# A four-layer graph network on one core: VectorE, GpSimd and SyncE in the order of the program, and one PSUM bank for each stage

## The chip, the core and the metric

The kernel runs on one core of one Trainium2 chip. The metric is the device time of one execution in microseconds, the median of several. The core has a matrix engine (TensorE, PE in the profile, with its weight loads PEld), a vector engine (VectorE, DVE), a scalar engine for activation functions (ScalarE, ACT), GpSimd (POOL), and SyncE (SP), which issues the DMAs. Each engine takes its own queue of instructions in order; semaphores tie them together. Matmuls write to PSUM, which has eight banks of 128 x 512 float32.

## The reference

The input is 64 graphs of 256 nodes with 128 features, `x` (64, 256, 128), and a 0/1 adjacency `adj` (64, 256, 256). Four layers follow each other, each with a residual and a layer norm:

```python
# layer 0: the maximum over the neighbours j of relu(p[i] + q[j] + b)
pre = p[:, :, None, :] + q[:, None, :, :] + b
h = jax.nn.relu(pre) * adj[..., None]
x = _layernorm(x + jnp.max(h, axis=2))
# layer 1: three elu branches, two products with adj, tanh
x = _layernorm(x + jnp.tanh(jnp.einsum('bnk,ok->bno', upd, W_upd) + b_upd))
# layer 2: two graph convolutions with D^-1/2 (adj + I) D^-1/2, elu between
x = _layernorm(x + out)
# layer 3: the sum over the neighbours j of gelu(layernorm(m_j[j] + m_i[i] + b1))
msg = jax.nn.gelu(_layernorm(pre, g1, be1), approximate=False)
agg = jnp.einsum('bijo,bij->bio', msg, adjacency)
x = _layernorm(x + _layernorm(jnp.concatenate([nodes, agg], -1) @ W2 + b2, g2, be2))
```

Layers 0 and 3 work on every edge. The kernel's sparse path handles them by sorting the nodes of a graph by degree and giving each node up to 40 slots for its neighbours.

## The kernel before, in words

**Four stages, pipelined over graphs.** All 64 graphs are unrolled. A graph goes through `first` (layer 0), `second` (layer 1), `third` (layer 2 and half of layer 3) and `last` (the rest of layer 3). In one round the kernel records `last` of graph g, `third` of g+1, `second` of g+2 and `first` of g+3 together. Each stage is a Python generator that stops at each `yield`; `together` always advances the stage that has done the smallest share of its steps, by the counts in `STAGES`. This gives the order in which instructions are recorded. A scheduler then reorders them for every engine, by its own estimate of when each could start, and puts in the waits.

**`first`** loads `xn` and `an`, makes `nz` and `diff` on DVE, transposes `nz` on PE into `aT` (copied by ACT), and counts neighbours (`pc`, `pd` in PSUM). From them come `kc`, `dg`, four Sign activations into `more` (L551), the place of each node (`place`, L556), and the permutation `perm` (L560, DVE). Matmuls with `perm` (L566) give `nzp`, then `rank` and `lack`, each a matmul and an ACT copy. `hot` (L629, DVE) is a 0/1 matrix of 4800 columns that says which node sits in which slot. The rows for the slots are gathered by three bf16 matmuls of `q3` with `hot` into a PSUM bank `bigp` (L665, L681 for the missing slots), and DVE folds the banks into `lanes` by the maximum (L492), ten banks for each half of the nodes. `permT` brings the maxima back (`m0`, L705 to L709), and a layer norm gives `x1`.

**`third` and `last`** gather in the same way for layer 3, in tiles of 1024 columns, ten for a graph. `sums_of` does one tile: gather on PE (L728), add the node's own term `dT` on DVE (L732, `pre`), square on ACT (L736), sum the squares over the features on PE (L743), copy them to `row` on ACT (L745), and write `row` to DRAM (`line`, L750). After two tiles, `vr` is read back with one variance for each edge (L762), brought to its inverse root, multiplied by `fu` (L769), written out (`scale_line`, L771), and later spread over all partitions by a DMA of 512 KB (`rs_s`, L828). `last` multiplies `pre` by `rs_s` (L839, DVE), applies Gelu (L841, ACT) and folds the sums (L492). The gather runs four tiles ahead of this (`AHEAD`), and `rs_s` two tiles ahead.

**Inverse roots** stand in five places: the variances `rs` of all layer norms, the degrees `dinv`, and `vr`. All call

```python
def inverse_root(t):
    nc.scalar.activation(t, t, AF.Sqrt)
    nc.vector.reciprocal(t, t)
```

ACT holds one table of functions at a time; where Sqrt, Exp and Gelu alternate, the built program has an ACT_TABLE_LOAD before the activation, shown under the line of the activation that follows.

**PSUM.** Four banks belong to the gathers (`bigp`, pool `ps_big`). The other four are one pool, `ps_mm`, under one name, `mm`, shared by all stages in turn.

Of the kernel before, what the change touches and what calls it, by code (L numbers as in the profile page):

```python
# [43 lines left out]
def kernel(  # L44
# [20 lines left out]
    half = consts.tile([P, N], F32, name="half")  # L65
    nc.vector.memset(half, 0.5)
# [4 lines left out]

    def inverse_root(t):

        nc.scalar.activation(t, t, AF.Sqrt)  # L74
        nc.vector.reciprocal(t, t)
# [81 lines left out]
    class Shared:  # L157


        def __init__(self, work, state, ps_mm):  # L160
            self.work, self.state, self.ps_mm = work, state, ps_mm

        def psum(self):
            return self.ps_mm.tile([P, 512], F32, name="mm")

        def layernorm(self, dst, src, g=None, be=None):

            st = self.work.tile([P, H, 6], F32, name="st", bufs=4)
            mv = self.work.tile([P, H, 2], F32, name="mv", bufs=4)
            for h in range(H):  # L170
                nc.vector.bn_stats(st[:, h], src[:, h])
                nc.vector.bn_aggr(mv[:, h], st[:, h])
            rs = self.work.tile([P, H], F32, name="rs", bufs=4)
            nc.vector.tensor_scalar(rs, mv[:, :, 1], EPS, None, ALU.add)
            yield
            inverse_root(rs)
            yield
            for h in range(H):
                if g is None:
                    nc.vector.tensor_scalar(  # L180
                        dst[:, h], src[:, h], mv[:, h, 0:1], rs[:, h:h + 1], ALU.subtract, ALU.mult
                    )
                else:
                    nc.vector.scalar_tensor_tensor(dst[:, h], src[:, h], mv[:, h, 0:1], g, ALU.subtract, ALU.mult)
                    nc.vector.scalar_tensor_tensor(dst[:, h], dst[:, h], rs[:, h:h + 1], be, ALU.mult, ALU.add)

        def elu(self, dst, t, twice=False):

            e = self.work.tile([P, 512], F32, name="elu_e")
# [6 lines left out]
            if twice:  # L196
                nc.vector.tensor_scalar(e, e, 1.0, None, ALU.min)
                nc.scalar.activation(e, e, AF.Exp, bias=minus1)
# [4 lines left out]
        def to_features(self, xn, name, bufs=None):  # L203

            pt = self.psum()
            for h in range(H):
                nc.tensor.transpose(pt[:, h * P:(h + 1) * P], xn[:, h], ident)
            t = self.state.tile([P, N], F32, name=name, **({"bufs": bufs} if bufs else {}))
            nc.scalar.copy(t, pt[:, :N])
            return t  # L210

# [3 lines left out]
        def layer_1(self, s, an, aT, x1):  # L215

            work, psum, elu = self.work, self.psum, self.elu
            xT = self.to_features(x1, "xT_1", 1)
# [6 lines left out]
            for h in range(H):  # L225
                nc.vector.tensor_add(io[:, h], pr[:, h * N:(h + 1) * N], b1_io)
            yield from elu(io, io)
# [5 lines left out]
            nc.vector.tensor_scalar(nd, pn[:, :N], b1_node, None, ALU.add)  # L233
            yield from elu(nd, nd)
# [16 lines left out]
            y = work.tile([P, H, P], F32, name="y", bufs=2)  # L251
            for h in range(H):
                nc.vector.tensor_add(y[:, h], pu[:, h * P:(h + 1) * P], b1_upd)
            nc.scalar.activation(y, y, AF.Tanh)
# [6 lines left out]
        def layer_2(self, s, aT, deg_of):  # L261
# [3 lines left out]
            deg = work.tile([P, H], F32, name="deg")  # L265
            deg_of(deg)
            nc.vector.tensor_scalar(deg, deg, 1.0, None, ALU.add)
            pos = work.tile([P, H], F32, name="pos")
            nc.vector.tensor_scalar(pos, deg, 0.0, None, ALU.is_gt)
            dinv = work.tile([P, H], F32, name="dinv")  # L270
            nc.vector.tensor_scalar(dinv, deg, 1e-30, None, ALU.max)
            inverse_root(dinv)
            yield
            nc.vector.tensor_mul(dinv, dinv, pos)
            for h in range(H):
                blk = aT[:, h, h * P:(h + 1) * P]
                nc.vector.tensor_add(blk, blk, ident)
            yield
            xT = self.to_features(x2, "xT_2", 1)
# [7 lines left out]
            for h in range(H):  # L287
                nc.vector.tensor_add(hs[:, h], ph[:, h * P:(h + 1) * P], b2[0])
            yield from elu(hs, hs, twice=True)
            yield  # L290
            for step in (1, 2):
                for h in range(H):
                    nc.vector.tensor_scalar(hs[:, h], hs[:, h], dinv[:, h:h + 1], None, ALU.mult)  # L293
# [17 lines left out]
                if step == 1:  # L311
                    yield from elu(hs, hs)
# [6 lines left out]
        def update(self, g, s, add_agg):  # L319
# [8 lines left out]
            y = self.work.tile([P, H, P], F32, name="y", bufs=2)  # L328
# [25 lines left out]
    def sparse(ctx):  # L354
        cs = ctx.enter_context(tc.tile_pool(name="cs", bufs=1))
        dram = ctx.enter_context(tc.tile_pool(name="dram", bufs=12, space=bass.MemoryType.DRAM))
        ps_mm = ctx.enter_context(tc.tile_pool(name="ps_mm", bufs=4, space=bass.MemoryType.PSUM))
# [32 lines left out]
        with tc.tile_pool(name="cs_prep", bufs=1) as pp:  # L390
# [21 lines left out]
            for t, slots in ((most, [w for s0, n, w in RECTS for _ in range(n)]), (least, SURE)):  # L412
# [7 lines left out]
                for hk in range(H):  # L420
                    pt = ps_mm.tile([P, 512], F32, name="mm")
# [7 lines left out]
            pt = ps_mm.tile([P, 512], F32, name="mm")  # L429
# [25 lines left out]
        sh = Shared(work, state, ps_mm)  # L455
        psum = sh.psum
# [37 lines left out]
        def split3(dst, src):  # L494

            r = work.tile([P, H, P], F32, name="rest")
            nc.scalar.copy(dst[:, 0], src)
# [3 lines left out]

        def first(g, s):

            xn = sh.node_tile("x0")
            nc.sync.dma_start(xn, x[ds(g, 1)].rearrange("b (h p) d -> p (b h) d", p=P))
            an = state.tile([P, H, N], F32, name="an")
            nc.sync.dma_start(an, adj[ds(g, 1)].rearrange("b (h p) j -> p (b h) j", p=P))
# [3 lines left out]
            nc.vector.scalar_tensor_tensor(diff, an, -1.0, an, ALU.add, ALU.mult)  # L511
            aT = state.tile([P, H, N], F32, name="aT", bufs=3)
            for hj in range(H):
                pt = psum()
                for hi in range(H):
                    nc.tensor.matmul(
                        pt[:, hi * P:(hi + 1) * P], nz[:, hi, hj * P:(hj + 1) * P], ident_b, start=True, stop=True
                    )
                nc.scalar.copy(aT[:, hj], pt[:, :N])
            nzT = as_bf16(aT)  # L520
            yield
            xT = sh.to_features(xn, "xT_0", 1)


            pd = psum()
            for h in range(H):
                cols = slice(h * N, (h + 1) * N)
                nc.tensor.matmul(pd[:, cols], many_b, nzT[:, h], start=True, stop=False)
                nc.tensor.matmul(pd[:, cols], ones_b[:1], down, start=False, stop=True)
# [9 lines left out]
            fl = work.tile([P, 1 + 2 * H * H], F32, name="fl")  # L539
            nc.scalar.activation(diff, diff, AF.Abs, accum_out=fl[:, 0:1])  # L540
            kc = work.tile([P, H, H], F32, name="kc")
            nc.vector.scalar_tensor_tensor(kc, pc, -1.0, down_c, ALU.mult, ALU.subtract)
            dg = state.tile([P, H], F32, name="dg", bufs=3)
            nc.vector.tensor_reduce(dg, pc, AX.X, ALU.add)
            s["dg"] = dg

            more = work.tile([P, H, H], F32, name="more")
            for h in range(H):
                for hi in range(H):
# [3 lines left out]
                    )  # L553
            yield
# [9 lines left out]
            for h in range(H):  # L564
                for hi in range(H):
# [3 lines left out]
                    )  # L569
            nzp = pair.tile([P, H, N], BF16, name="nzp")  # L570
            nc.scalar.copy(nzp, pz.rearrange("p (h n) -> p h n", h=H))
            permT = hold.tile([P, H, H, N], F32, name="permT")
            for h in range(H):
                pt = psum()
                for hk in range(H):
                    for hi in range(H):
                        nc.tensor.matmul(
                            pt[:, (hk * H + hi) * P:(hk * H + hi + 1) * P],
                            perm_b[:, h, hi, hk * P:(hk + 1) * P], ident_b, start=True, stop=True,
                        )  # L580
                nc.scalar.copy(permT[:, h].rearrange("p a n -> p (a n)"), pt)
# [3 lines left out]
            nc.tensor.matmul(pr, upto, nzp.rearrange("p h n -> p (h n)"), start=True, stop=True)  # L585
            rank = pair.tile([P, H, N], BF16, name="rank")
            nc.scalar.copy(rank, pr.rearrange("p (h n) -> p h n", h=H))
            pg = psum()
            nc.tensor.matmul(pg[:ROWS], ones_b[:, :ROWS], nzp.rearrange("p h n -> p (h n)"), start=True, stop=True)
            lack = hold.tile([ROWS, H, N], BF16, name="lack")  # L590
            nc.scalar.activation(
                lack, pg[:ROWS].rearrange("p (h n) -> p h n", h=H), AF.Relu, bias=part1[:ROWS], scale=-1.0
            )

            pf = psum()
            for h in range(H):
                for hk in range(H):
# [3 lines left out]
                    )  # L601
            yield
# [6 lines left out]
            lack_t = pair.tile([ROWS, H, g_n, g_w], BF16, name="lack_t")  # L609
            for h in range(H):  # L610
                nc.vector.tensor_mul(lack_t[:, h], tail, widen(lack[:, h, :g_w], g_n))
            s.update(an=an, aT=aT, perm=perm, permT=permT, lack=lack)

            full = pair.tile([ROWS, H, N], BF16, name="full")
            nc.vector.tensor_scalar(full, lack, 0.0, None, ALU.is_equal)
# [7 lines left out]
            yield  # L623

            hot = hold.tile([P, H, WIDTH], FP8, name="hot")
            for s0, n, w in RECTS[:-1]:
                for i in range(n):
# [4 lines left out]
                    if i % 4 == 3 or i == n - 1:  # L632
                        yield
# [9 lines left out]
            s["hot"] = hot  # L643

# [7 lines left out]
            q3 = work.tile([P, 3, H, P], BF16, name="q3")  # L652
            split3(q3, pq[:, :, 0])
            own = work.tile([P, H, P], F32, name="own")
            for h in range(H):
                nc.vector.tensor_add(own[:, h], pq[:, h, 1], b0s)
            yield
            mk = work.tile([P, H, H, P], F32, name="mk")
            for h in range(H):
                lanes = work.tile([P, 2, N], F32, name="lanes")  # L660
                for t0 in range(0, WIDTH, 512):
                    tl = min(512, WIDTH - t0)
                    pt = ps_big.tile([P, 512], F32, name="bigp")
                    for i in range(3):
                        nc.tensor.matmul(  # L665
                            pt[:, :tl], q3[:, i, h], hot[:, h, t0:t0 + tl], start=i == 0, stop=False
                        )
# [475 lines left out]
```

## Time and profile before

| what | value |
|---|---|
| median of 3 runs | 5728.43 us (5723.99 to 5739.29) |
| the profiled execution | 5731.62 us, span 5729.7 us |
| busy PE, DVE, ACT, POOL | 4529.9, 4834.4, 4275.2, 1.9 us |
| granted PE clock, mean | 0.862 |
| DMA | 365.15 MB, mean 64 GB/s |

The span runs from the first to the last instruction. In a row of a group, the line and engine are followed by the operation, out <- in by the program's names, the shapes, the count, then busy time and the mean of one in ns, and at last the time that the engine stood idle just before these instructions, with what ended it. A row of waits gives who waited for whom, the total in us, how many times, and the longest.

### The profile page before, as it was taken

The page shows a single profiled execution, that of the slowest core. Times are in us where ns is not written, and L with a number is a line of the kernel's source. Part 1 is how long each engine was busy: PE and PEld are TensorE (multiplying, and loading weights), DVE is VectorE, ACT ScalarE, POOL GpSimd, SP SyncE. Part 2 cuts the span into 40 slices and gives each one's busy share as a digit, 9 for nine tenths or more (in the row PEclk, how much of TensorE's full clock was granted, in tenths as well). Part 3 has the DMA queues.
Part 4 walks back from the last instruction along what each step waited for, and adds up shares of the span by engine and source line. Part 5 has one row for each costly group of instructions (what it writes and reads, how often), then busy time and mean ns, then how long its engine had stood idle before and what let it go on. Part 6 is the DMA issues. An engine that isn't in the chain of part 4 may idle for free.

```text
span 5729.7 us, 83531 instructions
## 1 busy us (share of the span) xinstructions
PE 4529.9 (79%) x27408; PEld 2508.7 (44%) x27408; DVE 4834.4 (84%) x14654; ACT 4275.2 (75%) x6485; POOL 1.9 (0%) x10
## 2 busy tenths in 40 slices
PE   5878878878778778788788788787887887877875
PEld 2444444444444444444444444444444444444443
DVE  6788888888888888888888888888888888888876
ACT  2577777777777777777777777777777777777785
POOL 0000000000000000000000000000000000000000
PEclk8888889889889889888898898898888887888986
DMA  0122222222212221221221222122212212221222
GB/s 22 44 70 63 62 63 72 62 63 66 69 57 70 65 63 63 72 63 62 63 72 62 63 65 70 59 68 65 63 62 72 64 62 63 69 66 60 68 65 74
DMA packets 292813, 365.15 MB, mean 64 GB/s; under 512 B 151952, under 2 KB 210448, under 8 KB 292368
## 3 DMA queue, kind: packets, MB, share of 16 engines
q1 hardware_dynamic: 292368, 359.73, 20.0%
q8 instruction: 217, 3.56, 0.3%
q14 instruction: 228, 1.87, 0.1%
HBM read 345.07 MB, written 14.53 MB: 63 GB/s over the span
## 4 chain that ended last, share of the span: by engine, by line
PE 52%; DVE 29%; ACT 11%; issue 4%; DMA 3%; SPq 0%; DVEq 0%; POOL 0%; ACTq 0%
PE bigp L665 11%; PE bigp L728 8%; DVE pre L839 6%; PE mm L860 5%; DVE lanes L492 4%; PE mm L743 4%; DVE hot L629 4%; DVE pre L732 4%; DVE sums L492 3%; PE bigp L681 3%; DMA rs_s<-scale_line 2%; PE mm L870 2%; PE mm L296 2%; PE mm L699 2%; PE mm L647 2%
## 5 line engine op out<-in xcount | busy, mean ns | idle before, releaser
L665 PE MATMUL bigp<-hot,q 128*128 128x512 fp8e4 (+1 forms) x3840 | 1052.3, 371 | 66.6 <-DVE lanes L492 52.6
L728 PE MATMUL bigp<-hot,c 128*128 128x512 fp8e4 (+1 forms) x3840 | 928.8, 372 | 140.2 <-DVE pre L732 140.2
L732 DVE TENSOR_TENSOR pre<-bigp,dT 128x512 f32<-128x512 f32 (+6 forms) x1664 | 846.3, 530 | 37.8 <-PE bigp L728 33.5
L492 DVE TENSOR_TENSOR lanes<-bigp,lanes 128x512 f32<-128x512 f32 (+6 forms) x1536 | 772.7, 503 | 94.6 <-PE bigp L681 86.9
L839 DVE TENSOR_TENSOR pre<-pre,rs_s 128x1024 f32<-128x1024 f32 (+1 forms) x640 | 732.9, 1150 | 48.6 <-DMA rs_s<-scale_line 48.0
L736 ACT ACTIVATE sq<-pre 128x1024 f32<-128x1024 f32 (+1 forms) x640 | 638.5, 998 | 169.9 <-DVE pre L732 163.9
L841 ACT ACT_TABLE_LOAD x535 | 686.4, 1283 | 9.5
L492 DVE TENSOR_TENSOR sums<-pre,sums 128x1024 f32<-128x1024 f32 (+6 forms) x1024 | 628.8, 614 | 41.2 <-ACT pre L841 40.7
L745 ACT ACTIVATE row<-mm,eps_t 128x256 f32<-128x256 f32 (+1 forms) x640 | 289.6, 453 | 476.9 <-PE mm L743 476.7
L841 ACT ACTIVATE pre<-pre,be,g 128x1024 f32<-128x1024 f32 (+1 forms) x512 | 594.2, 1172 | 57.8 <-DVE pre L839 53.0
L743 PE MATMUL mm<-sq,ones 128*32 128x256 f32 (+1 forms) x5120 | 482.9, 440 | 135.2 <-ACT sq L736 135.2
L74 ACT ACT_TABLE_LOAD x445 | 570.9, 1283 | 7.5
L728 PEld LDWEIGHTS <-c 128*128 128x128 bf16 x3840 | 331.2, 98 | 550.5 <-issue 136.1
L665 PEld LDWEIGHTS <-q 128*128 128x128 bf16 x3840 | 310.8, 97 | 392.6 <-issue 112.0
L296 PE MATMUL mm<-aT,hs 128*128 128x256 f32 x512 | 232.3, 600 | 316.1 <-DVE hs L293 214.8
L629 DVE TENSOR_SCALAR hot<-rank 128x512 fp8e4<-128x512 bf16 (+5 forms) x1536 | 440.5, 348 | 0.0
L681 PEld LDWEIGHTS <-pick 42*128 42x128 bf16 x2944 | 155.8, 95 | 481.5 <-issue 474.2
L296 PEld LDWEIGHTS mm<-aT,hs 128*128 128x128 f32 x512 | 135.6, 293 | 425.8 <-issue 316.1
L860 PE MATMUL mm<-w3u,sums 128*128 128x128 f32 x2048 | 296.7, 289 | 18.4 <-DVE sums L492 16.1
L194 ACT ACT_TABLE_LOAD x221 | 283.5, 1283 | 3.9
L681 PE MATMUL bigp<-lack,pick 42*128 42x36 bf16 (+16 forms) x2944 | 285.7, 187 | 0.0
L860 PEld LDWEIGHTS mm<-w3u,sums 128*128 128x128 f32 x2048 | 254.5, 195 | 37.3 <-issue 17.6
(226 smaller groups left out, 7132.6 us busy)
## 6 DMA issues: line engine op xcount, KB each, us to landing
rs_s<-scale_line SPq DMA_DIRECT2D x512, 512.0 KB
rs_s<-scale_line SPq DMA_DIRECT2D x128, 352.0 KB
an<-in_adj SPq DMA_DIRECT2D x64, 256.0 KB
x<-in_x SPq DMA_DIRECT2D x64, 128.0 KB
line<-row SPq DMA_DIRECT2D x512, 4.0 KB
out<-o SPq DMA_DIRECT2D x64, 128.0 KB
fu<-fulls SPq DMA_DIRECT2D x192, 4.0 KB
vr<-line SPq DMA_DIRECT2D x192, 8.0 KB
```

The costliest lines, as they stand in the source:

```text
L74: nc.scalar.activation(t, t, AF.Sqrt)
L492: nc.vector.tensor_tensor(lanes[:, :k, :w], src[:, i:i + k], lanes[:, :k, :w], op)
L629: nc.vector.tensor_scalar(hot[:, :, at:at + w], rank[:, :, :w], s0 + i + 1.0 - FAR, None, ALU.is_equal, saturate=False)
L665: nc.tensor.matmul(pt[:, :tl], q3[:, i, h], hot[:, h, t0:t0 + tl], start=i == 0, stop=False)
L681: nc.tensor.matmul(o_, l_, r_, start=False, stop=i == len(todo) - 1)
L728: nc.tensor.matmul(pt[:, :bl], c3[:, k, h], hot[:, h, t0 + b:t0 + b + bl], start=k == 0, stop=k == 2)
L732: nc.vector.tensor_add(block(pre[:, b:], n, w, at), block(pt, n, w, at), widen(dT[:, h, :w], n))
L736: nc.scalar.activation(sq[:, :tl], pre[:, :tl], AF.Square)
L743: nc.tensor.matmul(pr[q * Q:(q + 1) * Q, :tl // 4], ones[:, :Q], v4[:, :, q], start=True, stop=True)
L839: nc.vector.tensor_mul(pre[:, :tl], pre[:, :tl], rs[:, :tl])
L841: nc.scalar.activation(msg[:, :tl], pre[:, :tl], AF.Gelu, bias=be3, scale=g3)
L860: nc.tensor.matmul(pt[:, cols], lanes[:, k, cols], w3u[:, 1], start=k == 0, stop=False)
```

## The change

- **Order.** Recording of the sparse path now stands in `tc.manual_schedule` for DVE, Pool and SP: these three engines take their instructions in the order of the program. PE and ACT are still ordered by the scheduler.
- **Steps.** Many `yield`s are added, so that a step of a stage ends where its data change engine, and the counts in `STAGES` follow. Inside `first` the matmuls of the next bank are recorded a step before DVE folds the bank at hand, and the matmuls for `permT` and `xT` are spread between the comparisons for `hot`. `x` and `adj` are loaded at the end of the previous graph's `first`.
- **Tiles of layer 3.** `sums_of` is cut into `gather_tile`, `add_own`, `square_sums`, `squares_out` and `scales`. The gather runs five tiles ahead, `rs_s` one tile ahead with two buffers, not three. `sq` and `row` have one buffer, `pre` eight. The DMAs around `vr` are advanced one step at a time beside the stage (`with_chains`).
- **Inverse root.** It is a power of -0.5 on GpSimd. The products of `vr` with `fu` and of `dinv` with `pos` are on GpSimd too.
- **Degrees.** `dinv` is made in `first`; `third` multiplies `aT` by it once, where `hs` was multiplied before both convolutions.
- **PSUM.** `ps_mm` has one bank for each name, and each stage has its own name: `mm_f`, `mm_s`, `mm_t`, `mm_l`.

```diff
     def inverse_root(t):
-        nc.scalar.activation(t, t, AF.Sqrt)
-        nc.vector.reciprocal(t, t)
+        nc.gpsimd.tensor_tensor(t, t, mhalf[:t.shape[0], :t.free_size()], ALU.pow)
...
         def psum(self):
-            return self.ps_mm.tile([P, 512], F32, name="mm")
+            return self.ps_mm.tile([P, 512], F32, name="mm" + self.tag)
...
             nc.vector.tensor_scalar(rs, mv[:, :, 1], EPS, None, ALU.add)
-            yield
             inverse_root(rs)
+            yield
             yield
...
+            for h in range(H):
+                nc.vector.tensor_scalar(aT[:, h], aT[:, h], dinv[:, h:h + 1], None, ALU.mult)
...
             for step in (1, 2):
-                for h in range(H):
-                    nc.vector.tensor_scalar(hs[:, h], hs[:, h], dinv[:, h:h + 1], None, ALU.mult)
                 pa = psum()
...
-        ps_mm = ctx.enter_context(tc.tile_pool(name="ps_mm", bufs=4, space=bass.MemoryType.PSUM))
+        ps_mm = ctx.enter_context(tc.tile_pool(name="ps_mm", bufs=1, space=bass.MemoryType.PSUM))
...
+            dg = work.tile([P, H], F32, name="dg")
+            nc.vector.tensor_reduce(dg, pc, AX.X, ALU.add)
+            nc.vector.tensor_scalar(dg, dg, 1.0 / N, None, ALU.mult)
+            s["dinv"] = sh_f.inverse_root_of(dg, 4)
+            yield
+            pd = psum()
...
+            for k, (h, t0, tl) in enumerate(banks):
+                if k + 1 < len(banks):
+                    pts[k + 1] = fetch_tile(*banks[k + 1])
+                pt = pts.pop(k)
+                next(rest, None)
...
-        AHEAD = 4
+        AHEAD = 5
...
+            inverse_root(vr[:rows])
+            nc.gpsimd.tensor_mul(vr[:rows], vr[:rows], fu[:rows])
...
+            for i in range(len(TODO) + 1):
+                square_sums(s, i + AHEAD - 1, psum)
+                gather_tile(s, i + AHEAD)
+                if i < len(TODO):
+                    spread_scales(s, i + 1)
+                    h, t0, tl = TODO[i]
+                    pre, rs = s.pop(("pre", i)), s.pop(("rs", i))
+                    nc.vector.tensor_mul(pre[:, :tl], pre[:, :tl], rs[:, :tl])
+                    msgs[i] = msg = pre if t0 else big.tile([P, TILE], F32, name="sums")
+                    nc.scalar.activation(msg[:, :tl], pre[:, :tl], AF.Gelu, bias=be3, scale=g3)
+                    yield
+                if i + AHEAD - 1 < len(TODO):
+                    squares_out(s, i + AHEAD - 1)
+                    add_own(s, i + AHEAD)
+                    yield
...
-        STAGES = [(last, 34), (third, 34), (second, 14), (first, 44)]
+        IN_ORDER = ("DVE", "Pool", "SP")
+        STAGES = [(last, 35), (third, 42), (second, 18), (first, 58)]
...
+        with tc.manual_schedule(engines={mybir.EngineType[e] for e in IN_ORDER}):
+            if U == B:
+                steps(0)
```

## The prediction

> **What bounds the kernel now.** I read the busy times first, then the windows of one steady graph, then the rows of the operations that change, then the waits.
>
> ```profile
> span 5729.7 us, 83531 instructions
> PE 4529.9 (79%) x27408; PEld 2508.7 (44%) x27408; DVE 4834.4 (84%) x14654; ACT 4275.2 (75%) x6485; POOL 1.9 (0%) x10
> ...
> PE 52%; DVE 29%; ACT 11%; issue 4%; DMA 3%; SPq 0%; DVEq 0%; POOL 0%; ACTq 0%
> ```
>
> No engine is full: VectorE (DVE), the busiest, is idle 895 us, and the chain of waits changes engine all the time. One graph lasts 87.9 us: the stretch from 2000 to 4000 us holds 5210 of DVE's 14654 instructions, and 14654 / 64 = 229 belong to a graph, so 22.75 graphs ran in 2000 us. Start and end add 5729.7 - 64 x 87.9 = 104 us. Two windows of one graph:
>
> ```profile
> 2508.00:2556.00 48.00, 47.30 (x302) 26.21 (x301) 41.53 (x124) 34.17 (x49) 0.00 (x0) 0.98 0.22 66
> 2556.00:2596.00 40.00, 24.41 (x139) 13.88 (x138) 32.57 (x105) 34.20 (x56) 0.00 (x0) 0.74 0.18 57
> ```
>
> After the length come PE, weight loads, DVE, ACT, POOL, the granted clock and the DMA. For 48 us, while `first` gathers its maxima, PE is full (47.30) at clock 0.98. In the other 40 us PE does 24.41 at clock 0.74, DVE sits 7.4 us and ACT is busy 34.20. At clock 0.98 the whole graph would cost PE 47.3 + 24.41 x 0.74 / 0.98 = 65.7 us, so PE isn't the floor. DVE is, at 4834.4 / 64 = 75.5 us. What can be won is DVE's 12.4 us of waiting per graph, and the work taken off it.
>
> ```profile
> L841 ACT ACT_TABLE_LOAD x535 | 686.4, 1283 | 9.5
> L74 ACT ACT_TABLE_LOAD x445 | 570.9, 1283 | 7.5
> L194 ACT ACT_TABLE_LOAD x221 | 283.5, 1283 | 3.9
> L75 DVE RECIPROCAL vr<-vr 128x16 f32<-128x16 f32 (+1 forms) x320 | 78.4, 245 | 29.5 <-ACT vr L74 25.4
> L769 DVE TENSOR_TENSOR vr<-vr,fu 128x16 f32<-128x16 f32 (+1 forms) x320 | 52.9, 165 | 0.3
> L293 DVE TENSOR_SCALAR hs<-hs,dinv 128x128 f32<-128x128 f32 x256 | 61.0, 270 | 2.2
> ```
>
> A quarter of ACT's time is table loads, because the square root (L74) alternates with Gelu (L841) and Exp (L194).
>
> **Part by part: tables and the inverse root.** The root becomes a power on POOL. In the built order ACT's loads fall from 1236 to 379, six a graph: 857 x 1.283 = 1100 us off ACT, with 132 us of square roots (68.0 and 64.4), so ACT ends near 3040 us, 47 a graph. I count nothing for this directly: ACT is 11% of the chain and has slack already. The trace starts the next ACTIVATE 1.30 us after the load at 2564.17. The Trainium skill ("ScalarE: Activation LUTs", What ACT_TABLE_LOAD costs) adds a drain of some 1.38 us, 2.66 in all; no gap of that size stands after the load here. By its figure ACT would shed about 2.3 ms, an estimate from that page; the sum stays, since ACT sets no end.
>
> DVE loses the reciprocals (78.4 + 48.6 + 9.4), the products with `fu` (52.9) and the two on `dinv` (6.4 and 61.0): 256.7 us of rows. Neighbours overlap in the trace (a 0.25 us reciprocal starts at 2514.74, the next instruction at 2514.90), so I take 0.63 of it, 163 us. `aT` times `dinv` is added: 128 of 128x256, by the 0.29 us row of the `elu` tensor_scalar 37 us, 27 after overlap. Net -136 us, or -2.1 a graph: DVE 73.4.
>
> POOL gets 17 small operations a graph (11 powers, 6 products). No row shows a power. The nearest are POOL's set-up rows, 0.1 to 0.45 us each, 2 to 8 us a graph, off DVE. The latency counts at one place: in `first` only `o` (two of 0.33 us) lies between the variance and the normalised `x1`. Before, that path (root, reciprocal, waits) took from 2562.51 to 2565.76, 3.25 us. So the wait is 0 to 2.6 us; I take 1.0, nearer the short POOL rows. The skill speaks against this part ("SBUF — State Buffer", Who interferes with whom): POOL and a DVE instruction with two SBUF inputs share a read port, and one holds off the other. No row here shows it. Were every POOL operation to hold DVE for its whole length, 2 to 8 us a graph would go back, 130 to 510 us in all, an estimate from that page's rule.
>
> **DVE in program order.** This is the large unknown; the DVE order after is the same in every graph, so I laid before's rows along it and compared the work between two links of a chain with the time that the chain took.
> - `kc` to `place`: four Signs on ACT and the matmuls before them stand between. Before:
>
> ```profile
> 2568.96 0.16 DVE L542 SCALAR_TENSOR_TENSOR kc<-mm,down_c 128x4 f32<-128x4 f32 x1 [0.27 <-PE mm L534]
> ...
> 2576.26 0.16 DVE L556 TENSOR_SCALAR place<-more 128x4 f32<-128x4 f32 x1
> ```
>
>   That is 7.3 us, filled with other stages' work (DVE waited 0.7 us there in the whole run). After, four small ops, two adds of 0.66 and two of 0.24 lie between: 2.45 us. Bounds: 0 (ACT, relieved, does the Signs at once: 4 x 0.675 is 2.7) to 7.3 + 1.3 (`pd` now follows `kc`, four matmuls of 0.33) - 2.45 = 6.2. I take 4.5, since the built ACT order still has a square, a load and an Exp among the Signs. Behind `place` on DVE stand `perm`, then all stages; PE waits for `perm`.
> - `place` to `lack_t`: 7.9 us of DVE work against 4.8 us before; covered.
> - `q3` to the first maximum: a product of 1.22 and `x3` (0.6) against 3.3 us before (2511.6 to 2514.9): 1.5 us.
> - The rest: waits that keep their cause cost
>
> ```profile
> DVE lanes L492 <- PE bigp L681: 86.9, 172, 2.0
> DVE pre L839 <- DMA rs_s<-scale_line: 48.0, 57, 4.2
> DVE sums L492 <- ACT pre L841: 40.7, 67, 2.3
> DVE pre L732 <- PE bigp L728: 33.5, 103, 2.8
> DVE m L706 <- ACT m L705: 30.3, 64, 4.6
> DVE part_max L488 <- PE bigp L681: 25.8, 35, 1.0
> ```
>
>   together 265 us, 4.1 a graph. Steps that end at each change of engine, and the next bank's matmuls recorded one step earlier, should cover most; I take 1.5 and keep 0 to 4.1. `io L226 <- PE` (179.7), `rest L498 <- ACT` (93.4 and 22.1), `y L330` (72.1) and `fl L604` (51.0), 418 us, I count as gone: in the new order some 7.5 us of DVE work stand between the last `sums` and `y`, and a whole step or more at the others.
>
> Sum: 4.5 + 1.0 + 1.5 + 1.5 = 8.5 us, against 12.4.
>
> **PSUM and SP.** One bank a stage makes `first` wait for each copy before its next matmul; in that stage all but `pd` and the transposed `perm` hang on the copy by data already. `pd` is in the 6.2 above, `permT` is hidden behind 14 `hot` comparisons of 0.36 us; without that cover it costs 1.7 us. SP issues as many DMAs (2969 in the built program). `rs_s` is fetched one tile ahead, not two: 3.4 us from issue (2504.12) to use (2507.54) against some 8 us a tile. It now queues behind `line<-row`, which waits for ACT; the waits on `rs_s` are the 48.0 above. If all 640 products waited as those 57 do (0.84 us), 539 us would come; I take none beyond the 48.
>
> **Sum.** 73.4 + 8.5 = 81.9; x 64 = 5242; + 104 = 5346 us of span; + 1.9 (the profiled execution took 5731.62 in all) = 5348, which I round to 5350. That execution stands 3 us over the median of 5728.43.
>
> **Rivals.**
> - Full cover: the order leaves only the 4.1 us of kept waits. 64 x 77.5 + 104 = 5064. For it: ACT loses 19 us a graph, and both PE and DVE needs rise evenly along the new order. Against: 2.45 us can't cover four Signs.
> - Held queue (slower): DVE stands in order behind the serial chain of `first`, and nothing can overtake. Place: `kc`, `place`, `fl`, `rest`, the first `lanes`, `m0`. Price: 6.2 at `place`, half of the worst single waits at the five others (2.8, 2.7, 3.4, 2.0, 4.6: 7.8), and the 4.1: 73.4 + 18.1 = 91.5, or 64 x 91.5 + 104 = 5960. It decides from 14.5 us of waits a graph on. For it: PE already waits 4.11 us for `perm` in the window above, at half clock. Against: the chain measured 14.9 us (2566.2 to 2581.1) under a busier ACT, and 13.6 us of DVE work lie along it.
> - Waits are a matter of data, not of order: DVE keeps its 12.4 us. 64 x 85.8 + 104 = 5595.
>
> **Chances.** Forecast and its neighbours, 5200 to 5600 (the third rival among them): 0.55. Full cover, below 5200: 0.26. Held queue: 0.16. Within 0.3% of before (17 us, what a measurement of this kernel can tell): 0.03. So faster 0.55 + 0.26 = 0.81, same 0.03, slower 0.16. The range runs from 5060 (full cover) to 5640 (the third rival, with 0.7 us more a graph for POOL or SP); it leaves out the held queue and a little below. Faster cases alone: 5060 to 5600.
>
> **What would show it.** Right: about 379 table loads; ACT near 53%; DVE near 4700 us busy, some 88% of the span; the largest DVE wait on `place <- ACT sign`, 250 to 350 us, then the first `lanes`; PE's wait for `perm` still there. Wrong: a DVE wait on POOL above 100 us; DVE rows with two SBUF inputs (1.22 us for 128x1024) grown longer; PE full throughout; or waits above 14.5 us a graph.

## The result, and the profile after

The changed kernel takes **6257.99 us** (median of 3, 6244.23 to 6261.9) against 5728.43: a ratio of 1.0915, 95% interval 1.0879 to 1.095. The forecast was 5350 with a range of 5060 to 5640. It is wrong in sign, and the result lies beyond even the slower rival's 5960.

The head of the page of the changed kernel:

```profile
span 6242.5 us, 81758 instructions
...
PE 4959.5 (79%) x27408; PEld 2590.2 (41%) x27408; DVE 4992.3 (80%) x13438; ACT 3143.6 (50%) x4924; POOL 1544.2 (25%) x1098
```

ScalarE lost 1132 us, and 379 table loads are left. VectorE runs 1216 instructions fewer, yet is busy for *longer*: 4992.3 us where it was 4834.4. Its idle time went from 895 to 6242.5 - 4992.3 = 1250 us. So 158 us of busy time and 355 us of idle time make up the 513 us of span. The waits that end VectorE's idle time (total us, times, longest):

```profile
DVE lanes L501 <- PE bigp L714: 491.4, 329, 4.9
DVE place L575 <- ACT sign L569: 327.6, 64, 5.9
DVE pre L952 <- DMA rs_s<-scale_line: 83.4, 68, 4.3
DVE lack_t L618 <- ACT lack L604: 81.7, 64, 4.2
DVE x L180 <- POOL rs_f L75: 22.7, 64, 0.8
DVE rest L508 <- ACT q L505: 22.6, 34, 2.3
```

Compare with before: `lanes` 86.9, `lack_t` not in the list, and `place`

```profile
DVE place L556 <- ACT sign L551: 0.7, 1, 0.7
```

The waits for `io`, `y` and `fl`, which the forecast counted as gone, are gone or under 10 us. The new waits stand at three places, all in `first`. `lanes` is late at five folds of a graph, the same five in nearly every graph: 205 us in all at the first fold of the first half of the nodes, 43 at the next one, and 83, 16 and 142 at three folds in the middle of the second half.

Why is VectorE busy longer? Count times mean over the groups by form gives what its instructions last singly: 5715 us in all after and 5883 before, 168 less. But rows of neighbours overlap. Before, 5883 - 4834 = 1049 us of them lay on top of each other; after, 5715 - 4992 = 723. The timeline of the changed kernel shows where (start, length):

```profile
2560.58 0.41 DVE L508 TENSOR_TENSOR rest<-mm_t,c 128x256 f32<-128x256 f32 x1
2561.03 0.29 DVE L509 CAST c<-rest 128x256 bf16<-128x256 f32 x1
2561.36 0.43 DVE L510 TENSOR_TENSOR c<-rest,c 128x256 bf16<-128x256 f32 x1
2561.70 1.07 DVE L501 TENSOR_TENSOR lanes<-bigp,lanes 128x404 f32<-128x404 f32 x3
```

The CAST reads what its neighbour has just written, and starts 0.04 us after that one's end (2560.99). The next also needs its neighbour: 0.04 again. The `lanes` row does not need `c`; it starts 0.09 *before* that one's end. Over the whole trace, of the neighbours without a longer wait between them, 4367 read a tile that the one in front wrote (by its name, which does not tell the parts of a tile apart). The median from the end of the first to the start of the second is +0.034 us there, and -0.083 us in the other 8406. A dependent neighbour so costs 0.12 us: 0.083 of overlap that is lost, and 0.034 of idle time, too short for the list of waits, which starts at 0.15. Carrying a wait is not what costs: 3333 of the others carry one, for something done by then, and start early all the same.

The program's order is full of dependent neighbours: a statistic and its aggregate, the two steps of an `elu`, the three steps of a split. 4035 of them start after the end of the one in front, where 467 did before. (4035 - 467) x 0.083 = 296 us is an estimate of the overlap lost by them, for 326 measured. VectorE's gaps of up to 0.15 us add up to 155 us (48 before), its longer waits to 1090 (842 before). So the 513 us of span are -168 of rows, +326 of lost overlap, +107 of short gaps and +248 of waits: the waits are the smaller part.

With VectorE planned (a run below), the same aggregates have strangers between them:

```profile
2603.53 0.16 DVE L172 BATCH_NORM_AGGREGATE mv_t<-st_t 128x2 f32<-128x6 f32 x1
2603.61 0.25 DVE L689 TENSOR_TENSOR own<-mm_f,b0s 128x128 f32<-128x128 f32 x1
2603.78 0.17 DVE L172 BATCH_NORM_AGGREGATE mv_t<-st_t 128x2 f32<-128x6 f32 x1
2603.87 0.30 DVE L501 TENSOR_TENSOR sums<-pre,sums 128x180 f32<-128x180 f32 x1
```

Each of the last three starts 0.08 us before the end of the one in front.

A graph now lasts 96.3 us (4360 of VectorE's instructions ran from 2000 to 4000 us, and 210 belong to a graph). Its two windows (length, PE, weight loads, DVE, ACT, POOL, clock, DMA share, GB/s):

```profile
2500.00:2548.00 48.00, 30.33 (x131) 14.59 (x132) 38.92 (x111) 31.92 (x50) 18.92 (x12) 0.74 0.29 87
2548.00:2596.00 48.00, 45.54 (x299) 25.24 (x297) 39.02 (x100) 17.23 (x27) 5.68 (x6) 0.98 0.12 36
```

TensorE's full stretch (the maxima of `first`) is as long as before, 48 us at clock 0.98; VectorE is idle for 9.0 us of it (6.5 before). The other stretch grew from 40 to 48 us, still at clock 0.74; VectorE is idle there for 9.1 us (7.4 before).

### The profile page after: what moved, and what is told of

It reads as the page before. It is cut to its first block, busy times and chain, and to the rows that moved or that the text cites. A ratio compares the mean times of both kernels' runs of the same rounds, so it can differ in the third digit from the quotient of the medians.

```text
span 6242.5 us, 81758 instructions
## 1 busy us (share of the span) xinstructions
PE 4959.5 (79%) x27408; PEld 2590.2 (41%) x27408; DVE 4992.3 (80%) x13438; ACT 3143.6 (50%) x4924; POOL 1544.2 (25%) x1098
## 5 line engine op out<-in xcount | busy, mean ns | idle before, releaser
L75 POOL TENSOR_TENSOR vr<-vr,mhalf 128x16 f32<-128x16 f32 (+1 forms) x320 | 1135.1, 3547 | 1340.7 <-DMA vr<-line 1338.6
L786 PE MATMUL bigp<-hot,c 128*128 128x512 fp8e4 (+1 forms) x3840 | 1086.5, 411 | 47.2 <-DVE pre L799 45.0
L952 DVE TENSOR_TENSOR pre<-pre,rs_s 128x1024 f32<-128x1024 f32 (+1 forms) x640 | 736.1, 1150 | 84.2 <-DMA rs_s<-scale_line 83.4
L799 DVE TENSOR_TENSOR pre<-bigp,dT 128x512 f32<-128x512 f32 (+6 forms) x1664 | 801.0, 532 | 1.2 <-PE bigp L786 1.0
L75 POOL TENSOR_TENSOR rs_s<-rs_s,mhalf 128x2 f32<-128x2 f32 x64 | 44.6, 697 | 2287.1 <-DVE rs_s L174 2287.1
L786 PEld LDWEIGHTS <-c 128*128 128x128 bf16 x3840 | 355.7, 105 | 583.9 <-issue 350.3
L814 PE MATMUL mm_l<-sq,ones 128*32 128x256 f32 (+1 forms) x3072 | 328.3, 443 | 91.9 <-ACT sq L803 91.8
L938 PE MATMUL mm_l<-w3u,sums 128*128 128x128 f32 x2048 | 372.4, 339 | 29.1 <-DVE sums L501 28.3
L938 PEld LDWEIGHTS mm_l<-w3u,sums 128*128 128x128 f32 x2048 | 339.6, 244 | 80.8 <-issue 37.1
L305 PE MATMUL mm_t<-aT,hs 128*128 128x256 f32 x512 | 236.6, 612 | 63.8 <-DVE hs L202 63.8
L823 ACT ACTIVATE row<-mm_t,eps_t 128x256 f32<-128x256 f32 x256 | 121.5, 475 | 294.5 <-PE mm_t L814 204.6
```

What stands on the lines that cost most here:

```text
L75: nc.gpsimd.tensor_tensor(t, t, mhalf[:t.shape[0], :t.free_size()], ALU.pow)
L786: nc.tensor.matmul(pt[:, :bl], s["c3"][:, k, h], s["hot"][:, h, t0 + b:t0 + b + bl], start=k == 0, stop=k == 2)
L799: nc.vector.tensor_add(block(pre[:, b:], n, w, at), block(pt, n, w, at), widen(s["dT"][:, h, :w], n))
L814: nc.tensor.matmul(pr[q * Q:(q + 1) * Q, :tl // 4], ones[:, :Q], v4[:, :, q], start=True, stop=True)
L938: nc.tensor.matmul(pt[:, cols], lanes[:, k, cols], w3u[:, 1], start=k == 0, stop=False)
L952: nc.vector.tensor_mul(pre[:, :tl], pre[:, :tl], rs[:, :tl])
```

## The experiments

Theories. T1: the fixed order of VectorE's queue costs the time, by (a) the wait for `lanes`, (b) the waits at `place` and `lack_t`, (c) the lost overlap. T2: the power on GpSimd. T3: one PSUM bank a stage. T4: SyncE's order. T5, formed on the way: the power makes the chain `line`, `vr`, `scale_line`, `rs_s` late.

**1. All engines planned.**

```diff
-        with tc.manual_schedule(engines={mybir.EngineType[e] for e in IN_ORDER}):
+        with ExitStack():
```

> The changed kernel with the scheduler again choosing the order on all engines; power on GpSimd, the PSUM banks, the early loads and the steps stay. Theories: (T1) the fixed order of VectorE's queue is what costs the 530 us (its new waits: lanes on TensorE +404 us, place +327 us, lack_t +82 us, and some 350 us of overlap between neighbouring VectorE instructions lost); (T2) the power on GpSimd costs it; (T3) one PSUM bank a stage costs it; (T4) SyncE in the program's order costs it. T1: 5350 to 5700 us, with lanes <- PE back under 150 us and place under 50 us. T2 and T3: still above 6100 us. T4: below 5800 us too, but then the next run stays above 6100.

5928.95 us, ratio to before 1.0366 (1.0343 to 1.039). It fits no theory alone: 329 us come back, and 200 stay. `place` fell to 3.2 us and `lanes` to 72.6, but others came up (VectorE's waits):

```profile
DVE pre L952 <- DMA rs_s<-scale_line: 549.8, 260, 6.0
DVE part_max L497 <- PE bigp L714: 106.8, 63, 5.2
```

**2. VectorE alone planned.**

```diff
-        IN_ORDER = ("DVE", "Pool", "SP")
+        IN_ORDER = ("Pool", "SP")
```

> The changed kernel with VectorE's order alone given back to the scheduler; GpSimd and SyncE stay in the program's order. T1: within 100 us of the run in which all engines are planned, 5350 to 5700 us. T4: above 6100 us. T2, T3: above 6100 us.

5724.25 us, ratio 0.9998 (0.9987 to 1.001). VectorE's order alone costs 534 us, all that the change lost; T1 holds, and T4 falls, since SyncE's order is still fixed here. (That this lies over 100 us below run 1, against my expectation, is for run 13.) Busy times, then VectorE's waits:

```profile
PE 4666.9 (81%) x27408; PEld 2550.7 (45%) x27408; DVE 4738.1 (83%) x13438; ACT 3254.8 (57%) x5048; POOL 1571.3 (27%) x1098
```

```profile
DVE pre L952 <- DMA rs_s<-scale_line: 284.9, 224, 4.9
DVE lanes L501 <- PE bigp L714: 126.5, 214, 1.7
...
DVE place L575 <- ACT sign L569: 3.2, 1, 3.2
```

The same 13438 VectorE instructions, rows of 5652 us, are 4738 us busy: 914 us of overlap, 191 more than in order. Idle time is 5727.0 - 4738.1 = 989 us, 261 less: short gaps are 47 us against 155, waits 936 against 1090. So of the 515 us of span, about 300 are dependent neighbours (191 of overlap, 108 of short gaps), 154 are waits, and 63 are rows that last a little longer in order.

**3. A product for the power.**

```diff
-        nc.gpsimd.tensor_tensor(t, t, mhalf[:t.shape[0], :t.free_size()], ALU.pow)
+        nc.gpsimd.tensor_tensor(t, *[mhalf[:t.shape[0], :t.free_size()]] * 2, ALU.mult)
```

> The changed kernel with a product of two constants in the place of each power on GpSimd (same count and shapes; all inverse roots have a wrong, constant value), order kept. GpSimd's busy time should fall from 1544 us to under 500 us. T1: 6150 to 6260 us, since VectorE waits for GpSimd only 23 us in all. T2: below 5900 us.

6227.75 us, ratio 1.0881 (1.0863 to 1.0899). This kernel leaves out the inverse roots: each is a constant. GpSimd's busy time falls by 1075 us, the time by 30, VectorE's busy time by 9. In the fixed order the power costs next to nothing; T2 falls as the cause of the loss.

**4. The kernel before with the power alone.**

```diff
+    mhalf = consts.tile([P, 16], F32, name="mhalf")
+    nc.vector.memset(mhalf, -0.5)
...
-        nc.scalar.activation(t, t, AF.Sqrt)
-        nc.vector.reciprocal(t, t)
+        nc.gpsimd.tensor_tensor(t, t, mhalf[:t.shape[0], :t.free_size()], ALU.pow)
...
-            nc.vector.tensor_mul(vr[:rows], vr[:rows], fu[:rows])
+            nc.gpsimd.tensor_mul(vr[:rows], vr[:rows], fu[:rows])
```

> The kernel before with the power on GpSimd alone (inverse_root and the product with full), everything else planned as before. T1: the power is a gain that the order hides: ScalarE's busy time falls by about 850 us (table loads 963 to some 200 or 400), VectorE's rows by about 100 us; time 5450 to 5700 us. T2: slower than 5728 us, by up to 500 us.

5920.27 us, ratio 1.0343 (1.0326 to 1.036): T1's gain is missed, and in this kernel the power does cost, as T2 has it. (The kernel before has 1236 table loads, not 963; here 381 are left.) ScalarE's busy time fell by 1155 us and VectorE's by 71, and the kernel became 196 us slower. VectorE's longest wait, and GpSimd's rows by form (busy us, mean ns, idle time before):

```profile
DVE pre L841 <- DMA rs_s<-scale_line: 429.6, 217, 5.7
```

```profile
L77 POOL TENSOR_TENSOR vr<-vr,mhalf 128x16 f32<-128x16 f32 x192 | 571.0, 2974 | 582.5 <-DMA vr<-line 582.5
L77 POOL TENSOR_TENSOR vr<-vr,mhalf 108x16 f32<-108x16 f32 x128 | 458.1, 3579 | 1715.4 <-DMA vr<-line 1715.4
```

Before, the root of `vr` took 0.216 us on ScalarE and its reciprocal 0.246 on VectorE. The power takes 3 us or more, in the middle of a chain at whose end VectorE waits: 429.6 us for `rs_s` where it was 48.0. This is T5.

**5. `place` four steps later** (order fixed).

```diff
-            yield
-            yield
+            for _ in range(6):
+                yield
             pos = work.tile([P, H, H], F32, name="place")
...
-        STAGES = [(last, 35), (third, 42), (second, 18), (first, 58)]
+        STAGES = [(last, 35), (third, 42), (second, 18), (first, 62)]
```

> The changed kernel, VectorE's order still fixed, with four more empty steps between the Sign activations and `place` (so that VectorE's steps of the other stages come between; stage first counts 62). T1 (a fixed order costs where VectorE stands in front of work that isn't ready): the wait place <- ACT sign falls from 328 us to under 100 us and the time by 150 to 300 us, to 5950 to 6110 us. If the fixed order costs by the lost overlap of neighbours alone (T1c), or the wait only moves to the next place of the chain (lack_t, lanes), the time stays within 60 us of 6258.

6064.48 us, ratio 1.0588 (1.0571 to 1.0606): 194 us off. `place` fell to 8.9 us and `lanes` to 289.8, and a wait for the `elu` of `third` came up that was 6.9 (VectorE's waits):

```profile
DVE elu_e_t L197 <- ACT elu_e_t L194: 318.5, 64, 5.1
DVE lanes L501 <- PE bigp L714: 289.8, 341, 2.7
```

Both outcomes at once: the time falls as T1b says, and a wait of the old size stands at the next place. All of VectorE's waits of over 0.15 us fall from 1090 to 896 us, about the whole gain.

**6. Two steps for each bank of the fold** (order fixed).

```diff
                     rest = largest(h, lanes)
                     next(rest)
                 yield
+                yield
             for _ in rest:
...
-        STAGES = [(last, 35), (third, 42), (second, 18), (first, 58)]
+        STAGES = [(last, 35), (third, 42), (second, 18), (first, 78)]
```

> The changed kernel, order still fixed, with two steps instead of one for each of the 20 banks of the max fold (stage first counts 78), so that the fold takes 40 of 78 parts of the period instead of 20 of 58 and TensorE's work is spread. T1a (VectorE waits for lanes because TensorE has too much in the fold phase): lanes <- PE falls from 491 us to under 250 us, time 5950 to 6150 us. Against it: the front phase is squeezed into less of the period, and place and lack_t may wait longer; then the time stays within 60 us of 6258 and the sum of the waits lanes, place and lack_t stays near 900 us.

5910.67 us, ratio 1.0321 (1.0304 to 1.0339): 347 us off, more than expected. VectorE's waits:

```profile
DVE place L575 <- ACT sign L569: 179.0, 64, 3.2
DVE elu_e_t L197 <- ACT elu_e_t L194: 171.5, 64, 3.8
DVE lanes L501 <- PE bigp L714: 127.9, 104, 3.3
```

With the fold spread, `lanes` falls by 364 us, and TensorE's busy time from 4959.5 to 4735.6 at a mean clock of 0.873 instead of 0.836. T1a holds for the wait. The 347 us are not the worth of `lanes` alone: `place` fell by 149 with the same edit, and all waits together by 307, from 1090 to 783. Not an instruction was changed, only how four stages interleave. What stays of the loss is not waiting: run 6 waits 153 us less than run 2, and its span is still 183 us longer, by 186 us less overlap, 104 more of short gaps and 46 of longer rows.

**7. VectorE planned, the root of `vr` back on Sqrt and reciprocal.** Run 2's edit, and

```diff
-            inverse_root(vr[:rows])
-            nc.gpsimd.tensor_mul(vr[:rows], vr[:rows], fu[:rows])
+            nc.scalar.activation(vr[:rows], vr[:rows], AF.Sqrt)
+            nc.vector.reciprocal(vr[:rows], vr[:rows])
+            nc.vector.tensor_mul(vr[:rows], vr[:rows], fu[:rows])
```

> VectorE planned, GpSimd and SyncE in order, and the root of `vr` (the five 128x16 powers a graph, 3.0 to 3.9 us each) back on Sqrt and reciprocal, the small 128x2 powers left on GpSimd. The run with VectorE planned stood at 5724 us with pre <- DMA rs_s 285 us. T5 (the slow powers lengthen the chain line, vr, scale_line, rs_s, and VectorE waits at its end): rs_s under 120 us, time 5500 to 5650 us. If instead the table loads that come back (up to 640 of 1.28 us) hurt ScalarE's work on the path: 5720 us or more.

5841.81 us, ratio 1.0203 (1.0186 to 1.022): slower than run 2 by 118 us. The wait for `rs_s` fell to 51.2 us, as T5 says, but other waits took its place. VectorE's two longest, and ScalarE's groups of table loads at Gelu and at the root:

```profile
DVE lanes L501 <- PE bigp L714: 287.6, 195, 3.8
DVE aT L285 <- PE mm_s L253: 148.8, 62, 3.0
```

```profile
L955 ACT ACT_TABLE_LOAD x382 | 490.1, 1283 | 6.8
L849 ACT ACT_TABLE_LOAD x256 | 328.4, 1283 | 9.0 <-DMA vr<-line 4.0
```

The loads rose from 503 to 828, 417 us. That they cause the new waits fits, but no run separates it from the new plan that any edit brings.

**8. VectorE planned, the chain tile by tile.** Run 2's edit, and

```diff
-        GROUP = 2
-        PIECE = 16
+        GROUP = 1
+        PIECE = 8
```

> VectorE planned, GpSimd and SyncE in order, powers on GpSimd, but the scale chain taken for each tile by itself (10 chains of 128x8 a graph instead of 5 of 128x16; twice the small DMAs). T5: each power takes about half as long (some 2 us) and no tile waits for its neighbour: rs_s under 150 us, time 5550 to 5690 us. If the wait is the DMAs' own latency or SyncE's queue: rs_s stays above 230 us or grows, time 5720 us or more.

**5626.97 us**, ratio 0.9828 (0.9811 to 0.9844): 1.7% faster than the kernel before, and faster than the changed one. VectorE's waits, and the row of the power by form:

```profile
DVE sums L501 <- ACT pre L954: 216.3, 70, 4.0
DVE lanes L501 <- PE bigp L714: 110.1, 134, 3.4
...
DVE pre L952 <- DMA rs_s<-scale_line: 65.4, 81, 3.8
```

```profile
L75 POOL TENSOR_TENSOR vr<-vr,mhalf 128x8 f32<-128x8 f32 x512 | 955.9, 1867 | 2708.7 <-DMA vr<-line 2707.3
```

A power of 1.87 us, on a tile that waits for no neighbour, takes 220 us off the wait and 97 off the time, although GpSimd is busier (1686.9) and the chain's DMAs are twice as many. No run separates the shorter power from the neighbour that is not waited for. 130 of the 220 us came back in the wait of `sums` for ScalarE (86.0 in run 2).

**9. Before, with the power and the chain tile by tile.** Runs 4 and 8's edits together.

> The kernel before with the power on GpSimd and the scale chain taken tile by tile (GROUP 1, PIECE 8); everything planned. With the power alone it stood at 5920 us with pre <- DMA rs_s 430 us. T5 (the 3 to 4 us powers of 128x16 lengthen the chain that ends in rs_s): rs_s under 200 us and time 5600 to 5750 us. If GpSimd hurts in another way (a slow port, small powers queued behind long ones): above 5850 us.

5695.24 us, ratio 0.9945 (0.9926 to 0.9963). The chain's grain alone takes 225 us off run 4, more than that had lost. `rs_s` is half of what it was, a little over what I expected:

```profile
DVE pre L841 <- DMA rs_s<-scale_line: 220.5, 111, 5.3
```

With run 4 (the power alone makes `rs_s` late) and run 7 (without it on `vr` the wait falls to 51 us), T5 is shown for the wait. Whether the power as such is now a small gain is not shown: no run takes the chain tile by tile with Sqrt and reciprocal.

**10. Halves apart** (order fixed): the same instructions, 12 dependent pairs a graph less.

```diff
             for h in range(H):
                 nc.vector.bn_stats(st[:, h], src[:, h])
+            for h in range(H):
                 nc.vector.bn_aggr(mv[:, h], st[:, h])
...
                     nc.vector.scalar_tensor_tensor(dst[:, h], src[:, h], mv[:, h, 0:1], g, ALU.subtract, ALU.mult)
+            if g is not None:
+                for h in range(H):
                     nc.vector.scalar_tensor_tensor(dst[:, h], dst[:, h], rs[:, h:h + 1], be, ALU.mult, ALU.add)
```

> The changed kernel, order fixed, the same instructions, but in each layer norm both statistics before both aggregates, and in the one with weights both first steps before both second ones, so that 12 pairs of neighbours a graph no longer depend on each other. T1c (a VectorE instruction that needs its neighbour's output starts 0.04 us after that one's end, any other 0.08 us before it): 12 x 64 x 0.12 = 92 us less VectorE busy time, and 40 to 92 us less time, 6165 to 6220 us. If the lost overlap doesn't count because VectorE waits anyway: within 20 us of 6258, with waits up by what busy time falls.

6203.68 us, ratio 1.0827 (1.0812 to 1.0842): 54 us off. Busy times:

```profile
PE 4914.3 (79%) x27408; PEld 2560.3 (41%) x27408; DVE 4938.9 (80%) x13438; ACT 3139.9 (51%) x4924; POOL 1540.6 (25%) x1098
```

VectorE is busy 53 us less, and the median time falls by as much. The late neighbours fall from 4035 to 3269. Their overlap comes back (781 us against 723) and the short gaps shrink (123 against 155): 90 us for 766 pairs, the 0.12 us of the gaps. Waits took 45 of them back (`rs_s` 132.2 where it was 83.4), so 0.07 us a pair is left in the time. T1c holds.

**11. Shared PSUM banks** (order fixed): every stage takes from one pool of four banks.

```diff
-            return self.ps_mm.tile([P, 512], F32, name="mm" + self.tag)
+            return self.ps_mm.tile([P, 512], F32, name="mm" if self.tag else "mm")
...
-        ps_mm = ctx.enter_context(tc.tile_pool(name="ps_mm", bufs=1, space=bass.MemoryType.PSUM))
+        ps_mm = ctx.enter_context(tc.tile_pool(name="ps_mm", bufs=4, space=bass.MemoryType.PSUM))
...
```

> The changed kernel, order fixed, with the four PSUM banks shared by all stages as before instead of one bank a stage. T1 and the prediction: nothing, 6200 to 6300 us. T3 (a stage with one bank must wait until ScalarE or VectorE has read it): below 6100 us.

6261.45 us, ratio 1.093 (1.0912 to 1.0949). T3 falls. TensorE's busy time fell by 209 us (4750.5) and the time did not move: TensorE's busy time as such is no bound in this order.

**12. The three mends together** (5, 6 and 10, order fixed, `first` counts 82).

> The changed kernel, order still fixed, with the three mends together: `place` four steps later, two steps for each bank of the fold, halves of the layer norms apart (stage first counts 82). Singly the first two gave -193 and -347 us. If the terms add (T1a, T1b, T1c apart): 6258 - 193 - 347 - 70 = about 5650 us. If VectorE's waits only move along the chain: 5750 to 5900 us, with a new wait (elu, kc or place) of over 200 us.

6041.08 us, ratio 1.0547 (1.0531 to 1.0563): 130 us *slower* than run 6 alone, outside both expectations. VectorE's waits:

```profile
DVE lanes L504 <- ACT lanes L742: 195.7, 62, 3.4
DVE lanes L504 <- PE bigp L717: 155.5, 123, 2.4
DVE place L578 <- ACT sign L572: 152.5, 64, 3.2
```

The mends do not add. `place` hardly gained on run 6, and the fold now waits 196 us for ScalarE's copy of the first bank (34.2 in run 6). The halves apart still give overlap (772 us against 728 in run 6), but the waits are 953 us against 783. In a fixed order each shift of one stage's steps meets those of the other three anew.

**13. SyncE alone in order**, VectorE and GpSimd planned: `IN_ORDER = ("SP",)`.

> The changed kernel with SyncE alone in the program's order; VectorE and GpSimd planned. With GpSimd in order too it stood at 5724 us (rs_s 285 us), with all planned at 5929 us (rs_s 550 us). If SyncE's order gives the 205 us (a DMA that waits doesn't stand in front of the next tile's, or stands behind fewer): 5700 to 5780 us, rs_s near 285 us. If GpSimd's does (small powers in front of long ones): 5880 to 5950 us, rs_s near 550 us.

5717.74 us, ratio 0.9976 (0.9962 to 0.999).

```profile
DVE pre L952 <- DMA rs_s<-scale_line: 277.8, 218, 5.4
```

SyncE's order alone gives back the 205 us between runs 1 and 2; GpSimd's adds nothing (6 us the other way). Each run is planned anew, so this is the worth of the order, not of one DMA in it.

**14. Run 8 with two steps a bank.** Edits 8 and 6 together.

> The version with VectorE planned and the chain tile by tile (5627 us) with two steps for each bank of the fold (stage first counts 78). If TensorE's bunched work costs a planned VectorE too (lanes <- PE 110 us, PE 83% busy): 5480 to 5600 us. If the scheduler has already spread it, as steps only set its order of record: 5600 to 5660 us.

5628.91 us, ratio 0.9816 (0.9796 to 0.9836): the same as run 8. What gave 347 us in a fixed order gives nothing with VectorE planned.

## Why the prediction was wrong

The medians make a ladder, in this order of steps: before 5728; the power 5920 (+192, late `rs_s`); the other edits, all planned, 5929 (+9); SyncE in order 5718 (-211); GpSimd in order 5724 (+6); VectorE in order 6258 (+534). The forecast had neither the power's loss nor SyncE's gain, and that these two cancel is luck. It went wrong on the last step, in two terms of its sum.

- **VectorE's work, 73.4 us a graph: measured 4992.3 / 64 = 78.0.** "I take 0.63 of it" priced overlap as a property of the rows taken away. It is a property of the order: the rows did fall, by 168 us (I had 220), but the order took 326 us of overlap from the rows that stayed. The term was -136 us and became +158. The order of VectorE's instructions after the change was there to be read, the gap of a dependent pair was in the trace before, and I never put the two together.
- **The waits, 8.5 us a graph: measured (1250 - 101) / 64 = 18.0**, 101 being the start and end as before (895 - 64 x 12.4). The short gaps of dependent neighbours are 155 / 64 = 2.4 of them, and no term held them. `place`, taken at 4.5 within 0 to 6.2, measured 5.1: right. `x1` on GpSimd, taken at 1.0, measured 0.35. `lanes`, 1.5 for the first maximum plus a share of the "rest" of 1.5, measured 7.7, 3.2 at the first fold and 4.4 at four others: the failed step is "should cover most". I laid VectorE's work along the new order and found enough of it on average. But a queue in order waits whenever the *one* bank that is next is late, and five were, in nearly every graph. `lack_t`, "covered", measured 1.3; `rs_s` 1.3.
- **The held-queue rival** had the right mechanism for the waits. That its 18.1 us meets the measured 18.0 is luck: 2.4 are short gaps, which it did not have, 4.4 stand at later folds, and of the five places beside `place` that it priced, four stayed under 0.4. Its 5960 lacks 64 x 4.6 = 294 us of VectorE's work, mostly the lost overlap; with that it reads 6254. I gave it 0.16, because 13.6 us of VectorE's work stood along a chain of 14.9: again a sum where the sequence counts. Its point of 14.5 us was passed.
- **The 418 us of waits counted as gone** did go: `io` and `fl` have left the list, `rest` and `y_l` are 22.6 and 9.2.
- **"PE isn't the floor"** fits run 11. But TensorE's rhythm is what VectorE waits for at `lanes`.
- **Table loads**: 379, and ACT's end within 104 us of the 3040 forecast. "ACT sets no end" holds for how busy it is (50%); but VectorE waits 328 us at `place` for ACT's Signs, and run 7 leaves open what more table loads do in another order.
- **The power**: 0.70 us for 128x2 and 3.92 (128x16, mean) in place of the 0.1 to 0.45 of the set-up rows. That cost 23 us at `x1`. What I did not price was its other chain, `vr`; it is covered in the changed kernel (`rs_s` 83 us with the power, 91 without in run 3) and costs 196 us in the kernel before (run 4).
- **PSUM, counted at nothing**: right (run 11). **SP "none beyond the 48"**: close in the changed kernel (83.4); that SyncE's order is worth 205 us when VectorE is planned I had not seen.
- **The shared port.** With 1075 us less on GpSimd, VectorE's busy time moved by 9 us (run 3), and its product of two SBUF tiles, `pre` by `rs_s`, has rows of 1.22 us (128x1024) in both runs. The 130 to 510 us worked out from the Trainium skill ("SBUF — State Buffer", Who interferes with whom) did not show on VectorE's side. GpSimd paid, as the last section shows.

## What to carry to other kernels

A fixed order must be judged by its sequence: walk it and ask of each instruction whether the one in front makes its input, and whether that input is there each time; sums of work along a chain hide both. Take the gap of dependent and independent neighbours from the trace before predicting any reordering, and price a slow operation on another engine by the longest chain that it sits in, not by the queue that it is freed from. And test the parts of a compound change apart: here a gain (SyncE's order) and a loss of about the same size (the power) lay under one large loss. Without VectorE's order the change is worth nothing (run 2); with the chain cut tile by tile as well, it beats both kernels (run 8).

## What the hardware showed that I had not expected

- **Two VectorE neighbours.** The second starts 0.034 us after the end of the first when it reads what that wrote, and 0.083 us before it otherwise; between the planned and the fixed order that made 191 us of overlap and 108 us of short gaps. The Trainium skill ("VectorE: DVE Perf Modes", The DRAIN you can't avoid) has an instruction wait until the pipe of the one in front is empty, and adds: "A next op that is not held starts earlier". The trace agrees with the early start. What that page calls held goes by where operands start, not by who reads whose output, and no run here varies that.
- **GpSimd's power** goes by the elements of a row: at the least 0.69 us for 128x2, 1.63 for 128x8 (mean 1.87) and 2.89 for 128x16 (means 3.0 to 3.9), where a product of 128x16 takes 0.22 at the least.
- **A long VectorE product of two SBUF tiles holds GpSimd, and not the other way round.** Run 3's products for the root of `vr` take 0.215 us (median) outside the rows of `pre` by `rs_s`. 66 of them start inside such a row of 128x1024; they take 1.06 us (median) and end 0.07 us after that row, which lasts 1.22 us with or without GpSimd beside it. One of them (start, length):

```profile
2701.59 1.22 DVE L952 TENSOR_TENSOR pre<-pre,rs_s 128x1024 f32<-128x1024 f32 x1 [1.50 <-DMA rs_s<-scale_line]
2701.84 1.04 POOL L75 TENSOR_TENSOR vr<-mhalf 128x16 f32<-128x16 f32 x1 [2.47 <-DMA vr<-line]
```

- **TensorE's busy time and clock change with the order.** The same 27408 matmuls kept TensorE busy for 4514 us in run 4 and 4960 us in the changed kernel, and the gathers of 512 columns at L786 took 423 ns on average (386 before, at L728). The mean granted clock lay between 0.83 and 0.89 over the runs, but it does not settle the busy time: it was 0.851 in run 4, and 0.890 in run 7 with 4577.5 us.
